# A four-layer graph network on one core: the first layer divides its sums by the row sums before they are turned, with the reciprocals laid out again through DRAM

## The chip, the core and the metric

The kernel runs on one core of a Trainium2 chip. The core has five engines that run side by side: TensorE (PE, matrix products into PSUM), VectorE (DVE), ScalarE (ACT), GpSimd (POOL) and SyncE (SP, which here only issues DMAs). The metric is the device time of the whole program in microseconds. Three runs of the kernel before the change took 2767.30, 2769.96 and 2769.73 us; the median is 2769.73 us.

## What is computed

The reference applies four graph layers to 4096 nodes with 256 features, each as `x = layernorm(x + layer(x, adj))`. The change touches the first one, an additive attention with four heads:

```python
def _L0_gnn_ref(h, adj, W, a):
    ...
    Wh = (h @ W).reshape(n, heads, d)
    s_i = jnp.einsum('nhd,hd->nh', Wh, a[:, :d])
    s_j = jnp.einsum('nhd,hd->nh', Wh, a[:, d:])
    e = s_i[:, None, :] + s_j[None, :, :]
    e = jax.nn.leaky_relu(e, negative_slope=0.2)
    e = jnp.where((adj == 0)[:, :, None], -jnp.inf, e)
    alpha = jax.nn.softmax(e, axis=1)
    out = jnp.einsum('ijh,jhd->ihd', alpha, Wh).reshape(n, heads * d)
    return jax.nn.elu(out)
...
x = _layernorm(x + _L0_gnn_ref(x, adj, L0_gnn_W, L0_gnn_a), axis=-1)
```

## The kernel before

The first layer, `additive_heads`, goes over 8 blocks `b` of 512 destination nodes (`QW`), and within a block over 32 tiles `j` of 128 source nodes. One pair (b, j) is a unit. For a unit, `weights` makes the attention weights of four heads as a tile `prob` of 128 x 2048: ACT makes it head by head from `row` (lines 311 and 313), and DVE multiplies it by the adjacency `mask` and brings in the other branch of the leaky ReLU (line 328; for the four tiles `APART` = 3, 11, 19, 27 head by head, line 319). `sums` then multiplies `V` by `prob` on PE into three PSUM banks, `acc[b]` (line 338): two banks of sums of values and one of row sums; for the tiles of `APART` the row sums are left out, collected by DMA in `den` and added at the end of the block (line 342). PE runs `LAG` = 2 units behind in the program; there are 7 buffers of `prob` (`ga_z`) and 4 of `mask` (`ga_mask`, two tiles each), and what these allow sets how far ACT and DVE may run ahead of PE.

The end of block b is worked off during block b+1, in steps tied to j of that block (`finish`). First three copies move `acc[b]` to SBUF as `kept` (lines 344 to 346, one on ACT and two on DVE). At j = 4 and 10 PE turns two node tiles each by six 128 x 128 transposes into PSUM (`turned`, line 353); the row sums are turned with the values. At j = 4 PE also turns the sources of block b+2 (`rows`, line 292), which ACT copies to `line` and SP sends to DRAM (`far`, four small DMAs, line 297) and reads back broadcast as `row` (line 299). At j = 4, 7, 10, 13 DVE takes reciprocals of the turned row sums, multiplies and adds the positive part to X (`outputs`, lines 358, 360, 232), a node tile at a time; at j = 11, 14, 17, 20 ACT takes the exponential and DVE adds min(exp, 1) and the statistics (`add_exponential`, lines 238, 239, `one_row`, lines 156 and 157). At j = 22 and 24 comes the root of the variance (`begin_root`: DVE line 182, ACT lines 161 and 162; `end_root`: DVE lines 168 to 171), from j = 25 on the scaling of the rows (line 186). The last block has no later block to hide in; its end runs in `tail`, in the prologue of the second layer.

Only PE's order is written out by hand; the order on DVE, ACT, SP and POOL is made by a scheduler from the program and its dependencies, and each engine and each queue then works strictly in that order. Masks are issued by SP (line 306) as their buffers come free. POOL issues the `den` DMAs (lines 323, 325) and, behind each, one that narrows a part of the adjacency to bytes for the second layer (line 1380).

Of the kernel before, what the change touches and what calls it, by code (L numbers as in the profile page):

```python
# [9 lines left out]
FP = mybir.dt.float32  # L10
# [3 lines left out]
AF = mybir.ActivationFunctionType  # L14
OP = mybir.AluOpType
# [13 lines left out]
def kernel(  # L29
# [32 lines left out]
    def pool(stack, name, bufs, **kw):  # L62
        return stack.enter_context(tc.tile_pool(name=name, bufs=bufs, reuse_waits="tile", **kw))
# [5 lines left out]

    ident = const.tile([P, P], FP, name="ident")  # L70
    make_identity(nc, ident)
    ones = const.tile([P, P], FP, name="ones")
    nc.vector.memset(ones, 1.0)

# [21 lines left out]
    def spread(pl, ap, dims, shape, name, eng):  # L96

        sb = pl.tile(shape, FP, name=name)
        eng.dma_start(sb, bass.AP(tensor=ap.tensor, offset=ap.offset, ap=[[0, P]] + dims))
        return sb  # L100
# [53 lines left out]
    def one_row(mv, k, y):  # L154
        st = fin.tile([P, 6], FP, name="bn")
        nc.vector.bn_stats(st, y)
        nc.vector.bn_aggr(mv[:, k, :], st)
# [7 lines left out]
    def end_root(v, r, n, eng=nc.vector):  # L165

        s = fin.tile([P, n], FP, name=f"s{n}")
        eng.tensor_tensor(s, r, r, OP.mult)
        eng.tensor_tensor(s, s, v, OP.mult)
        eng.tensor_scalar(s, s, -0.5, 1.5, OP.mult, OP.add)  # L170
        eng.tensor_tensor(r, r, s, OP.mult)  # L171
# [7 lines left out]
    def begin_root(mv):  # L179
        n = mv.shape[1]  # L180
        v = fin.tile([P, n], FP, name=f"v{n}")
        nc.vector.tensor_scalar_add(v, mv[:, :, 1], EPS)
        return v, first_root(v, n), n

    def scale_row(y, mv, r, k):
        nc.vector.tensor_scalar(y, y, mv[:, k, 0:1], r[:, k:k + 1], OP.subtract, OP.mult)

# [46 lines left out]
    def add_exponential(o, b, k, mv, seen=None):  # L234

        y = X[:, b * QB + k, :D]
        with tc.issue_after(getattr(seen, "ins", seen)) if seen is not None else nullcontext():
            nc.scalar.activation(o, o, AF.Exp)
        nc.vector.scalar_tensor_tensor(y, o, 1.0, y, OP.min, OP.add)
        one_row(mv, k, y)  # L240

    def additive_heads(a, H, slope, early, narrow, ahead):
# [9 lines left out]
        with ExitStack() as lay:  # L252
# [10 lines left out]
            rp = pool(lay, "ga_row", 2)  # L263
            zp = pool(lay, "ga_z", 7)
            sb = pool(lay, "ga_sb", 2)
            op = pool(lay, "ga_o", 4)
            mp = pool(lay, "ga_mask", 4)
            dp = pool(lay, "ga_den", 1)
            dr = pool(lay, "ga_dram", 2, space=bass.MemoryType.DRAM)
# [5 lines left out]
            def bank():  # L275
                return ps.tile([P, QW], FP, name="g")
# [13 lines left out]
            def rows(b, pr):  # L290

                nc.tensor.transpose(pr[:QB * H, :P], src[:, b * QB:(b + 1) * QB, :].rearrange("p k h -> p (k h)"), ident)
                line = sb.tile([QB * H, P], FP, name="line")
                nc.scalar.copy(line, pr[:QB * H, :P])
                far = dr.tile([H, QB, P], FP, name="far")
                for k in range(QB):
                    nc.sync.dma_start(far[:, k, :], line[k * H:(k + 1) * H, :])
                row[b] = rp.tile([P, H, QW], FP, name="row")
                nc.sync.dma_start(row[b].rearrange("p h i -> p (h i)"),
                                  far.rearrange("h k i -> (h k i)").unsqueeze(0).to_broadcast([P, H * QW]))  # L300

            def weights(b, j, rows=None):
                m = b, j // MJ
                if j % MJ == 0:
                    mask[m] = mp.tile([P, MJ, QW], I32, name="mask")
                    nc.sync.dma_start(mask[m], edges[:, j:j + MJ, b * QW:(b + 1) * QW])
                z = prob[b, j] = zp.tile([P, H, QW], FP, name="prob")
                for h in range(H):
                    r = rows[h] if rows else row[b][:, h, :]
                    if j in APART:  # L310
                        seen = nc.scalar.mul(z[:, h, :], r, dst[:, j, h:h + 1])
                    else:
                        seen = nc.scalar.activation(z[:, h, :], r, AF.Relu, bias=-1.0, scale=dst[:, j, h:h + 1])  # L313
                factors[b, j] = seen
                if rows:
                    keep_rows(rows)
                if j in APART:
                    for h in range(H):
                        nc.vector.scalar_tensor_tensor(z[:, h, :], z[:, h, :], V[:, j, D + h:D + h + 1],  # L319
                                                       mask[m][:, j % MJ, :], OP.max, OP.mult)  # L320
                    if j == APART[0]:
                        den[b] = dp.tile([P, H, QW], FP, name="den")
                        seen = nc.gpsimd.dma_start(den[b], z)
                    else:
                        seen = nc.gpsimd.dma_start(den[b], z, accum_op=OP.add)  # L325
                    narrow(seen)
                    return
                nc.vector.scalar_tensor_tensor(z, z, 1.0, mask[m][:, j % MJ, :].unsqueeze(1).to_broadcast([P, H, QW]),  # L328
                                               OP.add, OP.mult)

            def sums(b, j):
                if j == 0:
                    acc[b] = pa.tile([P, HC + 1, QW], FP, name="acc")
                for n in range(HC if j in APART else HC + 1):
                    for h in range(H):
                        lo = h * d + n * G
                        part = V[:, j, lo:lo + G] if n < HC else V[:, j, D + h:D + h + 1].to_broadcast([P, G])
                        nc.tensor.matmul(acc[b][h * G:(h + 1) * G, n, :], part, prob[b, j][:, h, :],  # L338
                                         start=(j == 0), stop=(j == NT - 1 and n < HC))
                if j == NT - 1:  # L340
                    for h in range(H):
                        nc.tensor.matmul(acc[b][h * G:(h + 1) * G, HC, :], ones[:, :G], den[b][:, h, :],
                                         start=False, stop=True)
                    kept[b] = [fin1.tile([P, QW], FP, name=f"kept{c}") for c in range(HC + 1)]
                    for c in range(HC + 1):
                        (nc.vector.tensor_copy if c else nc.scalar.copy)(kept[b][c], acc[b][:, c, :])
                    mvs[b] = fin.tile([P, QB, 2], FP, name="mv")

            def turned(bank, b, k):

                po = bank().rearrange("p (c f) -> p c f", f=P)
                for c in range(HC + 1):
                    nc.tensor.transpose(po[:, c, :], kept[b][c][:, k * P:(k + 1) * P], ident)
                return po

            def outputs(sb, po, b, k):
                rden = fin.tile([P, H], FP, name="rden")
                nc.vector.reciprocal(rden, po[:, HC, ::G])
                o = out[b, k] = sb.tile([P, D], FP, name="o")
                nc.vector.tensor_tensor(o.rearrange("p (h c e) -> p h c e", h=H, c=HC),  # L360
                                        po[:, :HC, :].rearrange("p c (h e) -> p h c e", h=H),
                                        rden.unsqueeze(2).unsqueeze(3).to_broadcast([P, H, HC, G]), OP.mult)
                add_positive(o, b, k)

            def finish(b, j):

                if j in (4, 10):
                    k = (j - 4) // 3
                    pos[b, k], pos[b, k + 1] = turned(bank, b, k), turned(bank, b, k + 1)
                    if k == 0 and b + 2 < NB:  # L370
                        rows(b + 2, pos[b, 0][:, HC + 1, :])
                if j in (4, 7, 10, 13):
                    k = (j - 4) // 3
                    outputs(op, pos[b, k], b, k)
                if j in (11, 14, 17, 20):
                    k = (j - 11) // 3
                    add_exponential(out[b, k], b, k, mvs[b], factors[b + 1, j + LAG])
                elif j == 22:
                    roots[b] = begin_root(mvs[b])
                elif j == 24:  # L380
                    end_root(*roots[b])
                elif j in (25, 27, 28, 30):
                    k = (25, 27, 28, 30).index(j)
                    scale_row(X[:, b * QB + k, :D], mvs[b], roots[b][1], k)

            def turn(b, bank=bank):
                if b + 2 < NB:
# [6 lines left out]
                groups = [(0, HC + 1, side), (HC + 1, 1, bank().rearrange("p (n f) -> p n f", n=1))]  # L394
                additive_values(xTs[b], b, groups, w_sb, V, src, dst, H, slope, APART)

            pos, roots, xTs, out, factors = {}, {}, {}, {}, {}
            LAG = 2
            units = [(b, j) for b in range(NB) for j in range(NT)]
            with tc.manual_schedule(engines={mybir.EngineType.PE}):  # L400
# [1057 lines left out]
```

## Time and profile before

| what | value |
|---|---|
| runs | 2767.30, 2769.96, 2769.73 us |
| profiled execution: its time / its span | 2767.82 / 2766.0 us |
| PE busy in the span | 2750.1 us (99%) |
| DVE, ACT, POOL busy | 84%, 61%, 39% |
| granted TensorE clock | 1.0 |
| line 338, the sums | 5888 records, two to a product |
| line 353, the turns | 96, 281 ns each |
| first layer | from the start to about 703 us |

The span is one execution as the profiler recorded it. A product in this precision shows as two records. Durations of successive instructions of one engine overlap by some tens of nanoseconds, so that the distance from start to start is the better measure of what one costs. The ends of matmuls are modelled, so PE's busy share alone does not prove that PE is what bounds the kernel.

### The profile page before, as it was taken

How to read it: one execution, taken by the hardware profiler on the slowest of the kernel's cores; microseconds unless marked ns; L12 is line 12 of the kernel's file. 1: busy time of each engine (PE TensorE's matmuls, PEld its weight loads, DVE VectorE, ACT ScalarE, POOL GpSimd, SP SyncE). 2: the span in 40 equal slices, each digit the busy share in tenths (PEclk: the TensorE clock that was granted, in tenths of full speed). 3: DMA queues.
4: the chain of work that ended last, by engine and by line, in shares of the span. 5: the costliest groups of instructions: out<-in, count | busy, mean ns of one | idle time of the engine just before them, and what ended most of it. 6: DMA issues, size and time to landing. Idle time of an engine off the chain costs nothing. (4 is left out here: it accounts for less than half of the span.)

```text
span 2766.0 us, 50161 instructions
## 1 busy us (share of the span) xinstructions
PE 2750.1 (99%) x19365; PEld 1444.9 (52%) x19365; DVE 2311.0 (84%) x3121; ACT 1696.6 (61%) x2660; POOL 1075.5 (39%) x1020
## 2 busy tenths in 40 slices
PE   9999999999999999999999999999999999999999
PEld 5333333333543333333333336888888777777776
DVE  8899999999777788887888888888888876677776
ACT  8899999999346666666666665565655422222222
POOL 0000000000049878878788786454455000000000
PEclk9999999999999999999999999999999999999999
DMA  8798998987449899898998988577778544454442
GB/s 236 150 191 189 194 196 191 189 188 168 97 117 191 180 190 187 189 190 183 194 187 186 193 178 208 155 203 212 190 197 236 108 76 76 77 81 80 76 70 45
DMA packets 279673, 445.48 MB, mean 161 GB/s; under 512 B 55321, under 2 KB 156169, under 8 KB 274442
## 3 DMA queue, kind: packets, MB, share of 16 engines
q0 software_dynamic: 108784, 216.29, 46.9%
q1 hardware_dynamic: 164280, 218.88, 26.8%
q10 hardware_dynamic: 6370, 7.10, 0.8%
q8 instruction: 152, 2.49, 0.4%
q14 instruction: 87, 0.71, 0.1%
HBM read 335.94 MB, written 39.40 MB: 136 GB/s over the span
## 5 line engine op out<-in xcount | busy, mean ns | idle before, releaser
L888 DVE TENSOR_TENSOR prob<-p,mask 128x1024 f32<-128x1024 f32 x512 | 619.3, 1222 | 162.7 <-ACT p L878 157.0
L878 ACT ACTIVATE p<-p,shift 128x1024 f32<-128x1024 f32 x512 | 555.6, 1088 | 319.7 <-PE p L876 319.1
L338 PE MATMUL acc<-prob,V 128*32 128x512 f32 x5888 | 638.1, 593 | 1.2 <-DVE prob L328 1.1
L898 POOL TENSOR_TENSOR den<-den,prob 128x1024 f32<-128x1024 f32 x220 | 557.6, 2534 | 89.8 <-DVE prob L888 87.1
L313 ACT ACTIVATE prob<-row,dst 128x512 f32<-128x512 f32 x892 | 557.9, 711 | 3.3 <-PE acc L338 2.8
L876 PE MATMUL p<-qT,kT 64*64 64x512 f32 x4096 | 531.5, 591 | 2.3 <-DVE prob L888 2.3
L912 PE MATMUL acc<-prob,V 64*64 64x512 f32 x4096 | 530.1, 589 | 0.0
L328 DVE SCALAR_TENSOR_TENSOR prob<-prob,mask 128x2048 f32<-128x2048 f32 x224 | 507.4, 2285 | 12.6 <-ACT prob L313 11.7
L338 PEld LDWEIGHTS acc<-prob,V 128*32 128x32 f32 x5888 | 189.1, 110 | 434.1 <-issue 407.2
L484 PE MATMUL acc<-mix,mixed 128*128 128x256 f32 x1476 | 401.4, 380 | 1.9 <-DVE quarters L506 1.0
L912 PEld LDWEIGHTS acc<-prob,V 64*64 64x64 f32 x4096 | 157.6, 133 | 281.9 <-issue 280.1
L484 PEld LDWEIGHTS acc<-mix,mixed 128*128 128x128 f32 x1476 | 279.1, 190 | 45.3 <-PE acc L484 3.1
L876 PEld LDWEIGHTS p<-qT,kT 64*64 64x64 f32 x4096 | 154.4, 133 | 279.3 <-issue 252.1
L1185 DVE TENSOR_TENSOR prob<-prob,mask 128x1024 f32<-128x1024 f32 x128 | 156.4, 1222 | 142.9 <-ACT prob L1176 142.9
L904 POOL DMA_DIRECT2D den<-prob x240 | 233.5, 973 | 63.7 <-DMA den<-prob 34.1
L484 PE MATMUL acc<-prob,X 128*128 128x256 f32 x984 | 252.9, 380 | 0.6 <-ACT quarters L498 0.6
L1104 POOL DMA_DIRECT2D mask<-in_adjT x64 | 47.6, 744 | 529.1 <-DVE prob L1185 510.3
L484 PEld LDWEIGHTS acc<-prob,X 128*128 128x128 f32 x984 | 186.8, 190 | 79.8 <-issue 59.2
L617 DVE SCALAR_TENSOR_TENSOR prob<-r,own,mask 128x512 f32<-128x512 f32 x252 | 177.0, 743 | 48.1 <-POOL mix L476 11.9
L1176 ACT ACTIVATE prob<-p 128x512 f32<-128x512 f32 x144 | 86.1, 598 | 212.5 <-PE p L1172 212.5
L325 POOL DMA_DIRECT2D den<-prob x24 | 21.1, 878 | 475.7 <-DVE prob L319 475.7
L1176 ACT ACTIVATE prob<-g 128x512 f32<-128x512 f32 x112 | 66.9, 597 | 199.3 <-PE g L1172 199.3
(245 smaller groups left out, 3044.7 us busy)
## 6 DMA issues: line engine op xcount, KB each, us to landing
mask<-in_adjT SPq DMA_DIRECT2D x254, 512.0 KB
den<-prob POOLq DMA_DIRECT2D x240, 512.0 KB, 5.4
den<-prob POOLq DMA_DIRECT2D x32, 1024.0 KB, 9.2
mask<-edges SPq DMA_DIRECT2D x512, 64.0 KB
mask<-in_adjT POOLq DMA_DIRECT2D x64, 512.0 KB, 5.7
edges<-in_adj POOLq DMA_DIRECT2D x32, 512.0 KB, 17.1
far<-squares SPq DMA_DIRECT2D x16, 512.0 KB
den<-prob SPq DMA_DIRECT2D x16, 512.0 KB
```

The source lines that it names most:

```text
L313: seen = nc.scalar.activation(z[:, h, :], r, AF.Relu, bias=-1.0, scale=dst[:, j, h:h + 1])
L328: nc.vector.scalar_tensor_tensor(z, z, 1.0, mask[m][:, j % MJ, :].unsqueeze(1).to_broadcast([P, H, QW]), OP.add, OP.mult)
L338: nc.tensor.matmul(acc[b][h * G:(h + 1) * G, n, :], part, prob[b, j][:, h, :], start=(j == 0), stop=(j == NT - 1 and n < HC))
L484: nc.tensor.matmul(acc[at][:, half * HW:(half + 1) * HW], w, a, start=(g == 0 and n in (0, 2, 3, 5)), stop=(g == NP - 1), skip_group_check ...
L617: nc.vector.scalar_tensor_tensor(z[:, n, :], r, ga.own[:, j:j + 1], mask[:, n, :], OP.add, OP.mult)
L876: nc.tensor.matmul(p[c * d:(c + 1) * d, r, :], kT[half, c, at:at + d], qT[half, c, cols], start=True, stop=True)
L878: nc.scalar.activation(p, p, AF.Exp, bias=shift)
L888: nc.vector.tensor_tensor(z, p, mask[m][:, j % MJ, :].unsqueeze(1).to_broadcast([P, KC, QW]), OP.mult)
L898: nc.gpsimd.tensor_tensor(to, to, flat, OP.add)
L904: nc.gpsimd.dma_start(to, flat, accum_op=OP.add)
L912: nc.tensor.matmul(acc[b][c][r * d:(r + 1) * d, :], V[half, j, r * d:(r + 1) * d], prob[b, j][half, r, :], start=(j == 0), stop=(j == NH - 1))
L1185: nc.vector.tensor_tensor(z, z, co.mask[b, 2 * g // MJ][:, lo:lo + 2, :], OP.mult)
```

## The change

Four things change, for all blocks but the last:

1. The row sums alone are copied from PSUM at the end of the block (`total`, on ACT). `inverse_sums`, a generator that is moved on at j = 31 of the block and at j = 7 and 11 of the next, sends one row of each head to DRAM (`there`, 8 KB), reads it back as 128 x 16 (`few`), takes the reciprocal on DVE after the weights of j = 9, sends it to DRAM (`back`) and reads it broadcast to 128 x 512 (`rden`, four DMAs of 64 KB); then DVE multiplies the two banks of values by it, from PSUM to `kept`, after the weights of j = 12. All of these DMAs are on SP.
2. The turns come at j = 12 and 14, four for two node tiles, into one bank, with the heads put in order by the output pattern; there is no turn of row sums. The turn of the sources of block b+2 stays at j = 4.
3. The positive part, the exponential and the sum are done for two node tiles at a time (128 x 512); steps are bound to instructions of the weights by `after`.
4. The root of the variance takes its small constant as ACT's bias (`eps`, a new constant that POOL sets), and its refinement is three DVE instructions instead of four; scaling comes at j = 28 to 31.

In the order that the scheduler makes of it, DVE has `few`'s reciprocal after unit j = 9 of the next block and the two multiplies after j = 15; PE has the turns after its sums of j = 12 and 14; DVE adds the positive parts after the weights of j = 18 and 20. SP has `there` between the sixth and seventh masks of the next block, `few` behind the seventh, then two masks, four `far`, `back`, the tenth mask, `row` and the four `rden`. Before, `row` stood behind the four `far`, with no mask between.

```diff
+    def root_of(mv):
+        n = mv.shape[1]
+        r = fin.tile([P, n], FP, name=f"r{n}")
+        nc.scalar.activation(r, mv[:, :, 1], AF.Ln, bias=eps)
+        nc.scalar.activation(r, r, AF.Exp, scale=-0.5)
+        return r
+
+    def finish_root(r, var):
+        s = fin.tile(list(r.shape), FP, name=f"s{r.shape[1]}")
+        nc.vector.scalar_tensor_tensor(s, r, -0.5, r, OP.mult, OP.mult)
+        nc.vector.scalar_tensor_tensor(s, var, EPS, s, OP.add, OP.mult)
+        nc.vector.scalar_tensor_tensor(r, s, 1.5, r, OP.add, OP.mult)
...
-            op = pool(lay, "ga_o", 4)
+            op = pool(lay, "ga_o", 1)
...
-                    kept[b] = [fin1.tile([P, QW], FP, name=f"kept{c}") for c in range(HC + 1)]
-                    for c in range(HC + 1):
-                        (nc.vector.tensor_copy if c else nc.scalar.copy)(kept[b][c], acc[b][:, c, :])
+                    total = fin1.tile([P, QW], FP, name=f"kept{HC}")
+                    nc.scalar.copy(total, acc[b][:, HC, :])
+                    if b < NB - 1:
+                        divided[b] = inverse_sums(b, total)
+                        next(divided[b])
+                    else:
+                        kept[b] = [fin1.tile([P, QW], FP, name=f"kept{c}") for c in range(HC)] + [total]
+                        for c in range(HC):
+                            (nc.vector.tensor_copy if c else nc.scalar.copy)(kept[b][c], acc[b][:, c, :])
...
+            def inverse_sums(b, total):
+                few = op.tile([P, H * QW // P], FP, name="few")
+                there, back = (dr.tile([H, QW], FP, name=name) for name in ("there", "back"))
+                spread = lambda t: t.rearrange("h (q r) -> (h q) r", r=H * QW // P)
+                nc.sync.dma_start(there, total.rearrange("(h g) i -> h g i", h=H)[:, 0, :])
+                nc.sync.dma_start(few, spread(there))
+                yield
+                with after(masked[b + 1, 9]):
+                    nc.vector.reciprocal(few, few)
+                nc.sync.dma_start(spread(back), few)
+                rdens[b] = op.tile([P, QW], FP, name="rden")
+                for h in range(H):
+                    nc.sync.dma_start(rdens[b][h * G:(h + 1) * G, :], back[h:h + 1, :].to_broadcast([G, QW]))
+                yield
+                kept[b] = [fin1.tile([P, QW], FP, name=f"kept{c}") for c in range(HC)]
+                with after(masked[b + 1, 12]):
+                    for c in range(HC):
+                        nc.vector.tensor_tensor(kept[b][c], acc[b][:, c, :], rdens[b], OP.mult)
+                yield
+
+            def turned_pair(bank, b, k):
+                po = bank().rearrange("p (k f) -> p k f", f=D)
+                for n in range(2):
+                    for c in range(HC):
+                        nc.tensor.transpose(po[:, n, :].rearrange("p (h c g) -> p c h g", h=H, c=HC)[:, c],
+                                            kept[b][c][:, (k + n) * P:(k + n + 1) * P], ident)
+                return po
+
+            def pair_exponential(po, b, k, seen):
+                y = X[:, b * QB + k:b * QB + k + 2, :D]
+                e = op.tile([P, 2, D], FP, name="e")
+                with after(seen):
+                    nc.scalar.activation(e, po, AF.Exp)
+                nc.vector.scalar_tensor_tensor(y, e, 1.0, y, OP.min, OP.add)
+                for n in range(2):
+                    one_row(mvs[b], k + n, y[:, n, :])
...
             def finish(b, j):
-                if j in (4, 10):
-                    k = (j - 4) // 3
-                    pos[b, k], pos[b, k + 1] = turned(bank, b, k), turned(bank, b, k + 1)
-                    if k == 0 and b + 2 < NB:
-                        rows(b + 2, pos[b, 0][:, HC + 1, :])
-                if j in (4, 7, 10, 13):
-                    k = (j - 4) // 3
-                    outputs(op, pos[b, k], b, k)
-                if j in (11, 14, 17, 20):
-                    k = (j - 11) // 3
-                    add_exponential(out[b, k], b, k, mvs[b], factors[b + 1, j + LAG])
-                elif j == 22:
-                    roots[b] = begin_root(mvs[b])
-                elif j == 24:
-                    end_root(*roots[b])
-                elif j in (25, 27, 28, 30):
-                    k = (25, 27, 28, 30).index(j)
-                    scale_row(X[:, b * QB + k, :D], mvs[b], roots[b][1], k)
+                if j == 4 and b + 2 < NB:
+                    rows(b + 2, bank())
+                elif j in (7, 11):
+                    next(divided[b])
+                elif j in (12, 14):
+                    k = j - 12
+                    po = pos[b, k] = turned_pair(bank, b, k)
+                    y = X[:, b * QB + k:b * QB + k + 2, :D]
+                    nc.vector.scalar_tensor_tensor(y, po, 0.0, y, OP.max, OP.add)
+                elif j in (19, 21):
+                    k = j - 19
+                    pair_exponential(pos[b, k], b, k, factors[b + 1, j + LAG])
+                elif j == 25:
+                    with after(factors[b + 1, 27]):
+                        roots[b] = root_of(mvs[b])
+                elif j == 27:
+                    finish_root(roots[b], mvs[b][:, :, 1])
+                if j >= 28:
+                    k = j - 28
+                    scale_row(X[:, b * QB + k, :D], mvs[b], roots[b], k)
```

## Prediction

> **What bounds the kernel now.** The page says PE 99%, and that ends of matmuls are modelled, so I first ask whether PE really sets the pace of the first layer. Busy times over one block's length, from the view by stretches:
>
> ```profile
> core 0: us, PE busy (x) PEld busy (x) DVE busy (x) ACT busy (x) POOL busy (x), PEclk, DMA share, GB/s
> 390.00:472.00 82.00, 82.00 (x765) 25.37 (x758) 81.15 (x80) 79.65 (x135) 6.41 (x8) 1.00 0.90 190
> ```
>
> PE, DVE, ACT and the DMA engines are all within a tenth of full: this view decides nothing. The timeline does, by two marks that come once in a block: PE's products with `den` (line 342, end of a block) and DVE's first weights of `APART` (line 319, unit j = 3 of the next block).
>
> ```profile
> 123.83 2.73 DVE L319 SCALAR_TENSOR_TENSOR prob<-prob,V,mask 128x512 f32<-128x512 f32 x4
> 128.34 1.04 PE L342 MATMUL acc<-den,ones 128*32 128x512 f32 x8
> ...
> 373.23 2.73 DVE L319 SCALAR_TENSOR_TENSOR prob<-prob,V,mask 128x512 f32<-128x512 f32 x4
> 373.80 1.04 PE L342 MATMUL acc<-den,ones 128*32 128x512 f32 x8
> ...
> 455.62 1.04 PE L342 MATMUL acc<-den,ones 128*32 128x512 f32 x8
> 456.21 2.74 DVE L319 SCALAR_TENSOR_TENSOR prob<-prob,V,mask 128x512 f32<-128x512 f32 x4
> ...
> 619.26 1.04 PE L342 MATMUL acc<-den,ones 128*32 128x512 f32 x8
> 622.14 2.73 DVE L319 SCALAR_TENSOR_TENSOR prob<-prob,V,mask 128x512 f32<-128x512 f32 x4
> ```
>
> PE's mark comes every 81.82 us (373.80 to 455.62; over six blocks, 128.34 to 619.26, 81.82 as well): it never waits. DVE's comes every 82.98 us (373.23 to 456.21). DVE starts unit 3 4.5 us ahead of PE's mark in block 1, 0.6 ahead in block 4, 2.9 behind it in block 7. So **PE bounds the layer, and lives off a lead** that DVE and ACT build in block 0 and lose at 1.2 us a block. In time: PE begins unit 3 0.86 (line 342) + 3 x 2.58 = 8.6 us after its mark, a unit being six groups of four records at 0.43 (456.48 less 455.62, halved), or four groups, 1.72, in APART. DVE's unit 3 is ready that much less (start + 2.73) earlier: 10.4 us ahead in block 1, 6.4 in block 4, 3.0 in block 7. Ten is what seven buffers allow: ACT is then held by PE. Why DVE and ACT are slow, from the view of waits in 180 to 690:
>
> ```profile
> DVE prob L328 <- ACT prob L313: 3.5, 22, 0.2
> ...
> ACT r L161 <- DVE v L182: 15.6, 7, 2.4
> ```
>
> Once a block ACT waits 2.2 to 2.4 us for DVE's variance, and DVE then has little to wait for. ACT without that wait would need 80.6 a block.
>
> **PE's part of the change.** This is what counts as long as the lead holds.
>
> ```profile
> 456.48 12.20 PE L338 MATMUL acc<-prob,V 128*32 128x512 f32 x112
> 468.61 0.88 PE L353 MATMUL g<-ident,kept 128*128 128x128 f32 x6
> 469.32 0.27 PE L292 MATMUL g<-ident,src 128*16 128x128 f32 x1
> ...
> 485.11 0.87 PE L353 MATMUL g<-ident,kept 128*128 128x128 f32 x6
> 485.91 1.50 PE L338 MATMUL acc<-prob,V 128*32 128x512 f32 x12
> ```
>
> From 456.48 to the products' return at 469.52 it is 13.04 us, of which 28 groups take 12.04: six turns and the turn of sources cost 1.00. From there to 485.91 it is 16.39, of which 36 groups take 15.48: six turns cost 0.91. A turn is about 0.11, so going in and out costs 0.25 per place. After: two places of four turns, 0.69 each, and the turn of sources alone, 0.36 (it used to share a place): 1.74 against 1.91. That is 0.2 less in each of six blocks and, in block 7, which turns no sources, 1.82 less 1.38 = 0.4. **Sum 1.6 us.** The pattern that writes 4 x 32 instead of 128 in a row is in no row of the trace; a write of the same 128 elements I take at the same 0.11, with 0 to 0.1 more for each of 56 turns, at most 6 us, as ends. At the end of block 7 the lead is spent and PE loses some 0.2 us in its last units; that goes too: 1.8.
>
> **ACT's and DVE's part.** ACT: four exponentials of 256 become two of 512 (rows of 403 and near 711 ns with overlap: 0.31 and 0.61 from start to start), copies and small ones stay; the wait of 2.4 goes, as the statistics are done after j = 24 and the root stands behind j = 27. What is late next on ACT is only PE's release of a buffer. 80.6 a block. DVE loses two copies (0.60 each, 1.28 for the pair in the timeline with overlap) and four times a reciprocal, multiply, maximum and minimum (0.12 + 3 x 0.33): 5.6. It gains two multiplies, two maxima and two minima of 512 at 0.60 and a reciprocal of 16 at 0.15: 3.75. Statistics and scaling move, the root is one instruction shorter. 2 us less than its 81 busy: 79 to 80. Both are below PE's 81.6, so the lead stays near 10 us. None of it is on the path: worth nothing, apart from the 0.2 above.
>
> **What the change makes late: `rden`.** PE now needs `kept` after unit 12, and DVE makes it after unit 15, so the lead must cover three units. At a lead of 10.4, from PE's mark: PE's unit 13 starts at 0.86 + 11 x 2.58 + 2 x 1.72 + 0.36 = 33.0; DVE ends unit 11 at 28.7 - 10.4 = 18.3 and unit 15 at 39.6 - 10.4 = 29.2; the two multiplies make it 30.4. 2.6 us to spare, if `rden` has landed by 29.2, and 31.8 at the latest.
>
> The chain: ACT's copy of `total` ends at 0.86 + 0.9; `there` lands, `few` is issued, and so on. The price of a small write to DRAM is in the trace:
>
> ```profile
> 474.85 1.29 SPq L297 DMA_DIRECT2D far<-line  x4
> 478.38 0.35 SPq L299 DMA_DIRECT2D row<-far  x1
> ```
>
> 2.2 us from the end of the last issue to the dependent one. **Rule against row:** the Trainium skill, DMA: Bandwidth & Descriptors, Rules for kernel authors, says to coalesce small transfers, under 64 KB being mostly overhead, and its section Anatomy of one DMA — SWDGE (gpsimd) path fits 2.0 us of fixed time to a DMA of the software path. By it the four dependent hops cost 8 us, by the row 4 x 2.2 to 2.6, or 9 to 10; were they on the path, either would make seven blocks some 60 us slower. They are not: `few` lands near 8 (the sixth mask is ahead of it in the queue) and its reciprocal comes at 13; `back` lands near 17. The hop that matters is the last, since SP issues in order: the tenth mask (512 KB) waits until DVE has released unit 11, at 18.3; behind it are `row` (1 MB) and the four `rden` (256 KB). From then, 1 us to start and 1.8 MB, with the 1 MB that `den` adds at the same moment from POOL's queue. The view by stretches for the same mixture in block 5:
>
> ```profile
> 480.60:482.00 1.40, 1.40 (x18) 0.40 (x13) 1.40 (x1) 1.40 (x4) 1.11 (x2) 1.00 1.04 421
> 482.00:483.00 1.00, 1.00 (x16) 0.39 (x12) 1.00 (x2) 1.00 (x2) 0.58 (x1) 1.00 0.96 242
> 483.00:486.00 3.00, 3.00 (x34) 1.11 (x26) 3.00 (x3) 3.00 (x6) 0.00 (x0) 1.00 1.10 266
> ```
>
> At 421 GB/s (`row` alone) 1.8 MB takes 4.3 us; at 266, all 2.9 MB takes 10.9. So `rden` lands 5.3 to 12 us after unit 11's release; I take 9.5, as much of `den` comes last. DVE, held by the lead, is there after 10.9; free-running after four units of 2.2, 8.8. While DVE waits, all later weights wait; ACT and, for the lead, PE go on. What SP holds behind `rden` is a mask that cannot start before unit 13 is released anyway. The new DMAs add 0.28 MB to some 15.6 MB a block (190 GB/s x 82 us). `eps` on POOL comes before the first data: nothing.
>
> **The forecast:** 2767.8 (the profiled execution; its span is 2766.0) less 1.8 = 2766.0. The runs' median is 1.9 above that execution, which is one draw of the same spread, so I put the time at 2766.5. Less than 0.2% (5.5 us) can hardly be told from no change here, and this is well inside.
>
> **Rivals.** (1) *The wait for `rden` becomes the pace.* If it lands x us after the release, DVE needs 79.5 + (x - 8.8) a block; above x = 10.9 that passes PE's 81.6, the lead falls by the difference, the 2.6 to spare go, and PE waits at its turns. At x = 12.5, 1.6 a block: gone after about two blocks, then five times 1.6, +8: 2774; at 14, +20. For it: DMA share 0.9, above 1 in those stretches. Against: the lands worked out above. (2) *ACT and DVE stay as slow as they are* (another wait in place of the variance's), at 83.0: with turns that need a lead of 7.8, the lead of 10.4 is spent after two blocks and PE takes on 1.4 us in five: +5 after the gain, 2773. Against it: no other wait is seen. (3) *DVE was the pace already* and PE's fullness is modelled: then 83.0 to 81, seven times, -14: 2752. For it DVE's 99%; against it the two periods.
>
> **Chances.** Forecast 0.66, of which 0.02 at a time low enough to tell; (1) 0.21, of which 0.04 too small to tell; (2) 0.05; (3) 0.08. So faster 0.10, same 0.68, slower 0.22. Range: the forecast's own is 2763 to 2770 (median's spread and the turns' pattern); it reaches up to 2778 for (1) at x = 13, 2.1 a block from the second block on.
>
> **What would show it.** Right: line 342's marks 81.6 apart in blocks 1 to 6; DVE's line for j = 3 about 4.5 us ahead of them in every block; no wait of ACT at the root; no wait of PE at the turns. Wrong: DVE waiting for a DMA ahead of the multiplies by over 2 us in each block, PE idle before its first turn, or marks that follow DVE.

## The result and the profile after

| kernel | median us | runs | span of the profiled execution |
|---|---|---|---|
| before | 2768.92 | 6, from 2767.30 to 2770.11 | 2766.0 |
| after | 2789.95 | 6, from 2787.47 to 2791.08 | 2787.3 |

The ratio after to before is 1.0075, 95% interval 1.0062 to 1.0088: the change makes the kernel 21 us slower. That is rival (1) of the prediction, at about the price it had for x = 14 us. The time lies outside the prediction's range, which ended at 2778.

The busy times do not show it. One block of the changed kernel, from the view by stretches (columns as before: PE, PEld, DVE, ACT, POOL busy with their instructions, PEclk, DMA share, GB/s):

```profile
470.00:556.00 86.00, 83.45 (x757) 25.07 (x752) 79.59 (x67) 81.01 (x135) 6.39 (x8) 0.98 0.88 188
```

DVE does less work than before and ACT about what was forecast, and both sit in a block that is 86 us long. The granted clock, 1.00 everywhere in the first layer before, is 0.98 here. The timeline of PE shows where the block is stretched (a bracket holds the idle time ahead of a group and what ended it):

```profile
210.79 1.04 PE L358 MATMUL acc<-den,ones 128*32 128x512 f32 x8
211.65 12.20 PE L354 MATMUL acc<-prob,V 128*32 128x512 f32 x112
223.78 0.28 PE L308 MATMUL g<-ident,src 128*16 128x128 f32 x1
223.99 19.95 PE L354 MATMUL acc<-prob,V 128*32 128x512 f32 x184
247.66 1.41 PE L401 MATMUL g<-ident,kept 128*128 128x128 f32 x4 [3.72 <-DVE kept L390]
248.99 7.32 PE L354 MATMUL acc<-prob,V 128*32 128x512 f32 x48
256.24 0.65 PE L401 MATMUL g<-ident,kept 128*128 128x128 f32 x4
256.83 42.27 PE L354 MATMUL acc<-prob,V 128*32 128x512 f32 x392
298.91 1.04 PE L358 MATMUL acc<-den,ones 128*32 128x512 f32 x8
```

PE stands idle 3.72 us ahead of the first turn, until DVE has made `kept`. Outside this place and the twelve groups behind it (7.32 us) the block is what was forecast: two places of turns of 0.66 us, the turn of the sources alone, sums at 0.43 a group. The marks of line 358 come 83.69, 88.11, 83.31, 86.81, 86.12 and 85.56 us apart in blocks 1 to 6, against 81.82 before.

What DVE waits for, in the same block, by its timeline, and under it the issues of SP:

```profile
229.36 2.73 DVE L335 SCALAR_TENSOR_TENSOR prob<-prob,V,mask 128x512 f32<-128x512 f32 x4
...
246.82 1.29 DVE L390 TENSOR_TENSOR kept<-acc,rden 128x512 f32<-128x512 f32 x2 [5.01 <-DMA rden<-back]
```

```profile
232.12 0.39 SPq L322 DMA_DIRECT2D mask<-in_adjT  x1
232.69 0.33 SPq L315 DMA_DIRECT2D row<-far  x1
233.12 2.32 SPq L385 DMA_DIRECT2D rden<-back  x4
```

DVE releases unit 11 at 229.36 + 2.73 = 232.09; at 232.12 the tenth mask can leave, behind it `row` and `rden`. `rden` has landed at 246.82, x = 14.7 us after the release. In blocks 1 to 6 x is 14.7, 14.7, 13.9, 13.9, 14.7 and 14.4; the prediction took 9.5 and saw 12 as the end. (x is counted to DVE's start; in block 2 the last packet of `rden` came 1.8 us before it.) The view of waits from 128 to 690, for DVE, ACT and PE (us in total, times, longest):

```profile
DVE kept L390 <- DMA rden<-back: 31.2, 6, 5.9
```

```profile
ACT prob L329 <- PE acc L354: 12.9, 13, 2.7
ACT prob L329 <- DMA den<-prob: 12.0, 9, 2.0
```

```profile
PE g L401 <- DVE kept L390: 14.8, 11, 3.7
```

ACT's wait at the root is gone. In its place stands one that the prediction did not have: at unit 18, seven buffers after unit 11, ACT waits for the buffer that the `den` DMA of unit 11 is still reading (six of the nine waits; the other three stand at unit 2, seven after unit 27 of the block before). That DMA ends 12.4 to 13.4 us after its weights here, 9.0 to 10.7 before. Most of the difference is a later start: its first packet moves 5.4 to 5.7 us after the weights here, 2.7 to 4.0 before, though POOL issues it 0.3 us after them in both. Why it starts later is not shown.

**Where the 21 us are.** On PE: against a block of 81.62 us (the length that PE has where nothing waits, below) the six periods are 23.9 us too long. PE's waits at the turns are 14.8 of it: six of 1.2 to 3.7 us ahead of the first turn, and five of 0.2 within it. Another 6.8 follows the four longest waits: the twelve groups after the first turn took 7.32, 7.05, 7.05 and 6.85 us in blocks 2, 4, 5 and 6, and 5.36 in blocks 1 and 3. Of the remaining 2.3, some 1.9 lies in the first turns, which took 0.98 to 1.34 us from start to start, where a turn without a wait took 0.58. The view by stretches shows for block 2 why the groups were slow, in its PEclk, the third column from the right (one us a line: in the wait, in the twelve groups, and after them):

```profile
246.00:247.00 1.00, 0.00 (x0) 0.00 (x0) 0.18 (x1) 0.87 (x2) 0.00 (x0) 0.58 1.12 239
250.00:251.00 1.00, 1.00 (x12) 0.24 (x8) 1.00 (x2) 1.00 (x2) 0.00 (x0) 0.50 1.18 183
253.00:254.00 1.00, 1.00 (x15) 0.25 (x10) 1.00 (x1) 0.19 (x1) 0.00 (x0) 1.00 0.63 49
```

In this block the clock was halved while PE waited, and it came back only at the end of the twelve groups. What the turns save, 0.2 in each of six blocks and 0.8 in block 7 (82.43 against 83.19), leaves 21.9 of the 23.9; the spans differ by 21.3.

On DVE: it is busy 79.7 to 80.1 us in blocks 2 to 6 and waits 4.8 to 5.9 for `rden`, with a few tenths for `few` and ACT; its periods there are 85.1 to 86.1. That sets the pace, without any term for PE's clock. The halved clock is how PE spent a part of that time and, as far as the traces show, no further cost: after blocks 1 and 3, with the full clock, PE's next wait at a turn was 3.72 and 3.02 us; after blocks 2, 4 and 5, with the halved one, it was 1.23, 2.34 and 1.84.

**Why `rden` is so late.** The trace keeps every packet. `row` and `den` move in packets of 8 KB, the mask and `rden` in packets of 2 KB. In block 2:

| stretch | SP's queue | POOL's queue (`den`) |
|---|---|---|
| 233 to 237, mask and `row` | 256 packets of 2 KB, 58 of 8 KB | none |
| 237.6 to 240.8, `row` beside `den` | 53 packets of 8 KB | 54 packets of 8 KB, 628 ns each |
| 241.1 to 243.9, `rden` beside `den` | 51 packets of 2 KB | 62 packets of 8 KB, 628 ns each |

`row` and `den` move about equally many packets, as if they took turns, and so do `rden` and `den`, though `rden`'s packets are a quarter as large: it moves 37 GB/s beside 181. Its 128 packets are through at 245.0; `den`'s last packet starts at 244.7. The same stretches as a whole, by the view (GB/s in the last column):

```profile
234.00:238.00 4.00, 4.00 (x44) 1.19 (x39) 3.68 (x3) 4.00 (x7) 0.08 (x1) 1.00 1.04 291
238.00:241.00 3.00, 3.00 (x32) 0.91 (x28) 2.84 (x2) 3.00 (x6) 0.00 (x0) 1.00 1.04 270
241.00:244.00 3.00, 2.94 (x28) 0.65 (x20) 0.81 (x1) 3.00 (x6) 0.00 (x0) 1.00 1.03 226
```

From 233 to 245 the mean is 245 GB/s. That the size of the packets makes `rden` late, and not the bytes alone, is argued from these counts; no run isolates it.

### The profile page after: what moved, and what is told of

The parts are those of the page before. It is cut to its first block, busy times and chain, and to the rows that moved or that the text cites. A ratio compares the mean times of both kernels' runs of the same rounds, so it can differ in the third digit from the quotient of the medians.

```text
span 2787.3 us, 50094 instructions
## 1 busy us (share of the span) xinstructions
PE 2755.8 (99%) x19337; PEld 1439.9 (52%) x19337; DVE 2292.6 (82%) x3029; ACT 1700.3 (61%) x2647; POOL 1076.4 (39%) x1021
## 5 line engine op out<-in xcount | busy, mean ns | idle before, releaser
L354 PE MATMUL acc<-prob,V 128*32 128x512 f32 x5888 | 645.9, 598 | 1.1 <-DVE prob L344 1.1
L344 DVE SCALAR_TENSOR_TENSOR prob<-prob,mask 128x2048 f32<-128x2048 f32 x224 | 503.8, 2282 | 10.5 <-ACT prob L329 10.3
L552 PEld LDWEIGHTS acc<-prob,X 128*128 128x128 f32 x984 | 186.6, 190 | 79.6 <-issue 59.2
L685 DVE SCALAR_TENSOR_TENSOR prob<-r,own,mask 128x512 f32<-128x512 f32 x252 | 177.0, 743 | 50.8 <-POOL mix L544 13.1
L1244 ACT ACTIVATE prob<-p 128x512 f32<-128x512 f32 x144 | 86.1, 598 | 212.4 <-PE p L1240 212.4
```

The source lines that it names most:

```text
L344: masked[b, j] = nc.vector.scalar_tensor_tensor(z, z, 1.0, mask[m][:, j % MJ, :].unsqueeze(1).to_broadcast([P, H, QW]), OP.add, OP.mult)
L552: nc.tensor.matmul(acc[at][:, half * HW:(half + 1) * HW], w, a, start=(g == 0 and n in (0, 2, 3, 5)), stop=(g == NP - 1), skip_group_check ...
L685: nc.vector.scalar_tensor_tensor(z[:, n, :], r, ga.own[:, j:j + 1], mask[:, n, :], OP.add, OP.mult)
```

## Experiments

The ratios are to the kernel before, run on the same chip in the same session. "Lead" is how long ahead of PE's start on unit 0 of a block DVE has it done.

**`rden` ahead of `row`.**

```diff
 def rows(b, pr):
     ...
-    row[b] = rp.tile([P, H, QW], FP, name="row")
-    nc.sync.dma_start(row[b]..., far...)
+    def read():
+        row[b] = rp.tile([P, H, QW], FP, name="row")
+        nc.sync.dma_start(row[b]..., far...)
+    return read
 ...
-    rows(b + 2, bank())
+    reads[b + 2] = rows(b + 2, bank())
 elif j in (7, 11):
     next(divided[b])
+    if j == 7 and b + 2 < NB:
+        reads[b + 2]()
```

> `row` (1 MB) is read after the four `rden` DMAs on SP's queue in place of before them; `rden` is still behind the tenth mask. Theory A1 (`rden` is late because it stands behind `row` in its queue): `rden` lands 6 to 8 us after DVE releases unit 11 in place of 14.4, DVE hardly waits, 2765 to 2769 us. Theory A2 (the round trip through DRAM is too long, from the reciprocal after unit 9 on, whatever is in the queue): the landing moves by less than 2 us, 2784 to 2790 us.

Measured: 2778.98 us, ratio 1.0035 (1.0022 to 1.0048). Half of the loss, between the two theories. `rden` lands 10.2 to 11.2 us after unit 11's release in five blocks and 13.1 in one, so `row` was worth some 4 us of the 14.4. SP also took 3.3 to 3.6 us to issue the four `rden` in these five blocks, 2.1 to 2.4 in the changed kernel. But with another order the scheduler also put the multiplies one unit earlier, so that DVE still waits, and `den` is still there: in 235 to 239 the trace has 63 packets of `rden` beside 96 of `den`.

```profile
230.72 6.73 DVE L346 SCALAR_TENSOR_TENSOR prob<-prob,mask 128x2048 f32<-128x2048 f32 x3
241.04 1.29 DVE L392 TENSOR_TENSOR kept<-acc,rden 128x512 f32<-128x512 f32 x2 [3.59 <-DMA rden<-back]
```

Three units stand between the release of unit 11 (230.7) and the multiplies, where the changed kernel had four.

**The reciprocal one unit earlier.**

```diff
-                with after(masked[b + 1, 9]):
+                with after(masked[b + 1, 8]):
                     nc.vector.reciprocal(few, few)
```

> The reciprocal is bound to the weights of j = 8 in place of j = 9, 2.3 us earlier; with that the scheduler puts `back` and `rden` ahead of the ninth and tenth mask and of `row` on SP. Theory A1 (position in SP's queue): `rden` lands before DVE has done unit 12, no wait, 2764 to 2768 us. Theory A2 (length of the round trip alone): the landing is 2.3 us earlier, so DVE's wait falls from 5.3 to about 3 us a block, 2774 to 2780 us.

Measured: 2779.39 us, ratio 1.0038 (1.0023 to 1.0053). The wait for `rden` is gone, as A1 has it (the multiplies start 2.1 us after unit 11 in every block), and yet the time is A2's. Two other waits have come, in DVE's and ACT's views:

```profile
DVE few L381 <- DMA few<-there: 16.6, 7, 2.8
```

```profile
ACT prob L329 <- DMA den<-prob: 18.3, 5, 4.2
```

DVE comes to the reciprocal before `few` has landed, 2.2 to 2.8 us a block, because `few` is issued behind a mask. And the ninth and tenth mask and `row` now all stand behind `rden`, in the same stretch as `den`, which ends 12.1 to 13.3 us after its weights; ACT waits 3.1 to 4.2 us for its buffer in five blocks of six. DVE's and ACT's work is only 79.6 and 80.4 us a block, but with the waits it is 83.7 to 84.6; the lead falls to 1.4 and from block 4 on PE's marks follow at 83.8 to 84.6. So a second wait can set the pace when the one for `rden` is gone. Which of the two it is no run separates: in the last experiment DVE waits 1.4 to 2.6 us for `few` alone, and in that without a wait for `rden` ACT waits 0.5 to 2.1 us for `den`, and neither costs time.

**`den` in packets of 2 KB.**

```diff
-                        seen = nc.gpsimd.dma_start(den[b], z, accum_op=OP.add)
+                        for h in (0, 2, 1, 3):
+                            seen = nc.gpsimd.dma_start(den[b][:, h, :], z[:, h, :], accum_op=OP.add)
```

(and likewise for the first, without `accum_op`.)

> Each collecting DMA `den` (1 MB, packets of 8 KB) is issued as four DMAs of one head each (packets of 2 KB), the rest as in the changed kernel. Theory P (a DMA engine takes the packets of its two queues in turn, whatever their size, so that `rden`'s and the mask's 2 KB packets get a fifth of an engine while `den`'s 8 KB ones run): `row` gets four fifths and `rden` half, `rden` lands about 10 us after the release of unit 11, DVE's wait falls under 2 us, 2766 to 2773 us. Theory Q (only the sum of the bytes in that stretch counts): the landing stays at 13 to 15 us, 2786 to 2792 us.

Measured: 2782.97 us, ratio 1.0051 (1.0034 to 1.0068). `rden` lands 12.9 to 13.9 us after the release: hardly earlier, so P's number is missed. Q's landing holds within 0.1 us, its time is missed by 3. The edit changed more than the size of packets. SP needed 4.4 to 5.2 us to issue the four `rden` in place of 2.1 to 2.4,

```profile
403.44 4.51 SPq L387 DMA_DIRECT2D rden<-back  x4
```

and `den` started earlier: a head's DMA leaves when its weights are done, so that the first packet moves 0.2 us ahead of the release of unit 11, where it came 5.4 to 5.7 us behind it in the changed kernel. The tenth mask and `row` thus met `den` from the start. The packets of `den` took 176 ns and more for 2 KB, so that 1 MB was no faster. Whether smaller packets alone would have helped `rden` stays open.

**No wait for `rden`.**

```diff
-                        nc.vector.tensor_tensor(kept[b][c], acc[b][:, c, :], rdens[b], OP.mult)
+                        nc.vector.tensor_tensor(kept[b][c], acc[b][:, c, :], eps.to_broadcast([P, QW]), OP.mult)
```

> The multiplies take the constant `eps` as second operand in place of `rden`, so the sums of all blocks but the last are scaled by 1e-5 and not divided; every DMA is still issued in the same order. Theory A (DVE's wait for `rden` is the whole loss): line 358's marks 81.6 apart, no wait of PE at the turns, ACT and DVE ahead by the full seven buffers in every block, 2764 to 2768 us. Theory A+D (ACT's wait for the buffer that `den` of unit 11 still reads is a second cause, 1.2 to 2 us a block): the same time within 2 us, but ACT and DVE take 82.2 a block and the lead falls by some 0.6 a block. Theory B (the turns at units 12 and 14, or slower ACT and DVE, cost by themselves): over 2775 us.

Measured: 2769.05 us, ratio 0.9991 (0.9982 to 0.9999). All six marks are 81.62 apart, PE does not wait at a turn, and the order on PE and SP is that of the changed kernel. On DVE the scheduler put the multiplies after units 12 and 13, where the changed kernel has both after unit 15 (block 1):

```profile
147.40 2.29 DVE L344 SCALAR_TENSOR_TENSOR prob<-prob,mask 128x2048 f32<-128x2048 f32 x1
149.61 0.68 DVE L390 TENSOR_TENSOR kept<-acc,eps 128x512 f32<-128x512 f32 x1
150.21 2.28 DVE L344 SCALAR_TENSOR_TENSOR prob<-prob,mask 128x2048 f32<-128x2048 f32 x1
152.41 0.68 DVE L390 TENSOR_TENSOR kept<-acc,eps 128x512 f32<-128x512 f32 x1
```

That these earlier places are not what saved the time is shown by the next experiment, in which they stay after unit 15. With it B falls, and the loss of the changed kernel is DVE's wait. ACT's wait for `den`'s buffer stays, 0.5 to 2.1 us in five of the six blocks; it takes the lead from 10.3 to 6.2 in the first block and holds it near there (5.7 in block 7), because with less lead the wait is shorter. By itself it costs nothing here, which is less than the A+D line had.

**`den` after unit 13.**

```diff
-        APART = (3, 11, 19, 27)
+        APART = (3, 13, 19, 27)
```

> `APART` is (3, 13, 19, 27) in place of (3, 11, 19, 27): `den`'s second MB leaves after unit 13, some 4.5 us later, and SP's order stays as it is. Theory P (`rden` crawls because its 2 KB packets take turns with `den`'s 8 KB packets): only the tenth mask, `row` and `rden` share that stretch, `rden` lands 7 to 9 us after the release of unit 11, no wait, 2764 to 2769 us. Theory A1 (its place behind `row` is what counts): it lands after 12 us or later, 2782 to 2790 us.

Measured: 2769.65 us, ratio 0.9992 (0.9983 to 1.0). `rden` stands behind `row` as before, and the whole loss is gone:

```profile
231.50 2.73 DVE L335 SCALAR_TENSOR_TENSOR prob<-prob,V,mask 128x512 f32<-128x512 f32 x4
234.15 4.72 DVE L344 SCALAR_TENSOR_TENSOR prob<-prob,mask 128x2048 f32<-128x2048 f32 x2
238.79 1.28 DVE L390 TENSOR_TENSOR kept<-acc,rden 128x512 f32<-128x512 f32 x2
```

There is no bracket: DVE finds `rden` landed in four blocks of six and waits 0.4 and 1.0 in the others, where it comes at 9.7 and 10.3 us (forecast 7 to 9). From the issue of `rden` to the last packet of `row` it was 4.6 us in block 1 (7.4 in the changed kernel) and from there to the last of `rden` 0.9 (4.6). So `den` was worth over 6 us in that block, a little more than `row`. As an estimate, 1 MB at the 245 GB/s of the changed kernel would account for 4.3 of it; this run does not separate bytes from packets. `den` itself ends 9.1 to 10.6 us after its weights and ACT does not wait for it.

**The root alone, on the kernel before.**

```diff
-                elif j == 22:
-                    roots[b] = begin_root(mvs[b])
-                elif j == 24:
-                    end_root(*roots[b])
-                elif j in (25, 27, 28, 30):
+                elif j == 25:
+                    with tc.issue_after(...factors[b + 1, 27]...):
+                        roots[b] = root_of(mvs[b])
+                elif j == 27:
+                    finish_root(roots[b], mvs[b][:, :, 1])
+                elif j >= 28:
```

> The kernel before with the change's root alone: the constant as ACT's bias, root bound behind the weights of j = 27, three instructions of refinement, scaling at j = 28 to 31. By the prediction's step on ACT: ACT's 2.4 us wait goes, ACT and DVE keep their lead of 10 us in all blocks, PE stays the bound, 2766 to 2769 us (nothing that the time can tell). Rival (ACT's wait only moves elsewhere): the lead still falls by 1.2 us a block, same time.

Measured: 2770.11 us, ratio 0.9995 (0.9987 to 1.0004). The lead is 8.6 us in blocks 2 to 7 (forecast 10), where it fell by 1.2 a block before, ACT does not wait at the root, and the time is the same: the lead was not what bound the kernel.

**A set order on SP.**

```diff
+                    behind = fews.get(b - 1) if j == 12 else sent.get(b - 1) if j == 18 else None
+                    with (after(behind) if behind is not None else nullcontext()):
+                        mdma[m] = nc.sync.dma_start(mask[m], ...)
 ...
-                with after(masked[b + 1, 9]):
+                with after(masked[b + 1, 8]):
 ...
+                if j == 20 and b + 2 < NB:
+                    with after(mdma[b + 1, 11]):
+                        reads[b + 2]()
```

> The changed kernel with SP's order set: `few` right behind `there`, reciprocal after the weights of j = 8, `back` and `rden` ahead of the ninth mask, `row` read behind the twelfth mask (after unit 15). If `rden` and `den` are late only because they meet `row` and the masks: no wait of DVE for `few` or `rden`, `den` of unit 11 lands 9 us after its weights as in the kernel before, ACT does not wait for its buffer, lead 10 us in every block, marks 81.6 apart, 2763 to 2767 us, which is 2 us under the kernel before. If another cause is left: over 2772 us.

(`fews` and `sent` hold the DMA of `few` and the last of `rden`; `reads` is that of the first experiment.)

Measured: 2768.01 us, ratio 0.9988 (0.9981 to 0.9995): 3.5 us under the kernel before on that chip (2771.55). That is 0.12%, which is less than can be told well, though the interval leaves 1 out; the forecast of 2763 to 2767 is missed by 1. All marks are 81.62 apart and block 7 is 82.43. SP's issues in block 2:

```profile
222.61 0.34 SPq L386 DMA_DIRECT2D back<-few  x1
225.48 0.34 SPq L389 DMA_DIRECT2D rden<-back  x1
225.92 1.29 SPq L313 DMA_DIRECT2D far<-line  x4
227.25 1.23 SPq L389 DMA_DIRECT2D rden<-back  x3
228.58 11.40 SPq L326 DMA_DIRECT2D mask<-in_adjT  x4
240.03 0.47 SPq L316 DMA_DIRECT2D row<-far  x1
```

`rden` has left before the masks, and `row` 12 us after it. DVE waits neither for `rden` nor, through ACT, for `den` (which ends 9.4 to 10.5 us after its weights). Against the forecast, it still waits 1.4 to 2.6 us a block for `few`; that costs nothing, because the lead stays at 7.4 to 8.3.

## Why the prediction was wrong

- *What bounds the layer, and PE's part of the change:* right. PE's block is 81.62 us where nothing waits, forecast at 81.6; a place of four turns is 0.66 and the rearranging pattern costs nothing. Block 7 gained 0.8, forecast at 0.6.
- *DVE's and ACT's part:* right in size. DVE is busy 79.7 to 80.1 us in blocks 2 to 6, forecast 79 to 80; ACT's work without its waits is 81.0 to 81.4, and 80.4 where the reciprocal comes one unit earlier, forecast 80.6; its wait at the root goes. Wrong in one clause: that only PE's release of a buffer is late next on ACT. The buffers of `APART`'s units are also read by `den`'s DMAs, and these end some 3 us later in the changed kernel.
- *The chain through DRAM up to `back`:* right; `few` had landed within 0.7 us of the reciprocal, and only `rden` was awaited for long.
- *The landing of `rden`:* **this step failed.** The prediction put it 9.5 us after the release of unit 11, with 12 as the end, and it was 13.9 to 14.7. The bytes were all in the sum (1.8 MB from SP, 1 MB of `den`, at 421 to 266 GB/s), and the start took 1.06 us in block 2 as forecast. But 9.5 assumed that much of `den` comes after `rden`, and none did: its packets moved among `row`'s and `rden`'s, and SP's queue moved some 250 GB/s from 233 to 237, with `den` absent, and 136 beside it from 237.6 to 240.8. The end of 12 did put all 2.9 MB first and was passed as well, because the stretch moved at 245 GB/s and not at 266, which is 0.9 us, and because nothing stood in the sum for the time from the last packet to DVE's start, 1.8 us in block 2. With `row` taken out of the way `rden` came at 10.2 to 13.1 us, with `den` out of the way at 10.3 or earlier; with both in the way it is 14.4 in the mean.
- *Rival (1):* right. Its rule, 79.5 + (x - 8.8) a block, gives 85.1 at x = 14.4; DVE's periods in blocks 2 to 6 are 85.1 to 86.1. That its price of +20 at x = 14 comes so near the 21 measured is in part chance: it counts seven blocks, and six had the wait. It had a fifth of the chances because the bound of 12 was taken for the end of what `rden` could do. Its sum had no term for PE's clock, and needed none as long as DVE sets the pace.
- *Rivals (2) and (3):* in the changed kernel (2) does not show by itself, but the second experiment is (2) with other waits. (3) falls: in the experiment without a wait for `rden`, DVE's work is 79.8 us a block, and the time is that of the kernel before.

On coalescing small transfers, the rule of the Trainium skill that was weighed (DMA: Bandwidth & Descriptors, Rules for kernel authors): the fixed cost that it counts was not what hurt, since in the last experiment the four dependent hops are all still there and cost no time. The page has another passage that bears on this case (Queues, rings and completion order): each DMA engine goes round the queues that have work, a packet at a time. The table of packets agrees for `row` and `den` (53 to 54) and roughly for `rden` and `den` (51 to 62). The page counts 9 to 17 descriptors to a packet as typical; whether a packet of the trace is such a packet, no run here shows.

## What to carry to other kernels

A small transfer that an engine waits for must be looked at with what is ahead of it in its own queue and what the other queue sends in that moment; for an upper end, put all these bytes ahead of it, at the lowest rate that the trace shows for such a mixture, and add the time from the last packet to the engine's start (1.8 us in block 2 here). Set such a transfer off before the large ones, and move the one that has time (`row`, needed a block later) out of the way. When one wait is taken away, look for the next transfers that are late in the same stretch: they may become the pace.

## What the runs showed of the hardware

PE's clock fell to half after waits of PE of 1.5 to 3.7 us, and the length of a wait alone did not decide it. In the changed kernel, waits of 1.84, 2.34, 3.02 and 3.72 us ahead of the turns were followed by a granted clock of 0.50 for 3.4 us (6.8 after the longest), and those of 1.23 and 1.61 us were not; with `rden` ahead of `row`, 1.48 us was enough. First the wait that was not followed, then the one that was:

```profile
161.86 0.30 PE L401 MATMUL g<-ident,kept 128*128 128x128 f32 x1 [1.61 <-DVE kept L390]
```

```profile
494.24 0.30 PE L403 MATMUL g<-ident,kept 128*128 128x128 f32 x1 [1.48 <-DVE kept L392]
```

The clock's records in the traces explain the difference. All its changes stand whole multiples of 3.413 us apart: in the changed kernel it falls at 246.17, 420.25, 505.58 and 590.91 us, which is 51, 25 and 25 such steps. If PE's idle time, by its records, is counted in these fixed stretches, then in all nine traces, from 20 to 2750 us, each stretch at full clock with 1.69 us of it or more was followed by the half clock (ten of them), and none with 1.58 or less. The wait of 1.61 us lay across the border of two stretches; the wait of 1.48 lay in one, together with the 0.21 that came within the turn. So for these kernels the limit is about half of a stretch. The Trainium skill (TensorE: Matmul & The Clock Gate, HAM oscillation) speaks of gaps over some 3.4 us; here half of that sufficed, and the measurement decides. Where it was halved, twelve groups took up to 7.32 us in place of 5.36.
